# Half-size gather tables for the first pair, loads of x moved to GpSimd, and two extra matmuls before the first weight turn

## The chip, the cores and the metric

The kernel runs on one core of a Trainium2 chip. TensorE (PE) multiplies matrices, VectorE (DVE) and ScalarE (ACT) work on elements, GpSimd (POOL) issues the gathers, and SyncE (SP) and ACT issue plain transfers. The metric is device time in microseconds, lower is better: 733.51 us before the change (median of three runs, 733.4 to 733.7).

## The reference

Three layers of a compressed interaction network over B = 1024 rows, F = 39 fields, E = 64 embedding columns, H = 64 outputs a layer, all in float32:

```
def _cin_layer(Xk, X0, W, b):
    O = W.shape[0]
    Hk, Fdim = (Xk.shape[1], X0.shape[1])
    Wr = W.reshape(O, Hk, Fdim)
    return jnp.einsum('bhe,bfe,ohf->boe', Xk, X0, Wr) + b[None, :, None]
X0 = sparse_embedding
Xk = X0
outs = []
for W, b in ((W0, b0), (W1, b1), (W2, b2)):
    Xk = _cin_layer(Xk, X0, W, b)
    outs.append(Xk.sum(axis=-1))
cin_output = jnp.concatenate(outs, axis=-1)
return cin_output @ fc_w.T + fc_b
```

Only the sum over E of each layer and one dot product with fc_w leave the model, so the second and third layer can be folded into weights that act on products of two fields.

## The kernel before, in words

The 65,536 columns (b, e) are cut into 32 blocks of 2048. Every block needs products of pairs of fields. The products of a block fill six chunks of 128 rows (steps 0 to 5); what is left over, 32 rows of a half block, is done once for two blocks together, as step 6 of the even block (`join`). Two consecutive blocks are called a pair here; the first pair is blocks 0 and 1.

How a product is made: for each block GpSimd gathers five tiles of 128 rows of fields, `rt[n % 2][:, 0..4]`, out of a table in DRAM, by an indirect DMA with a column of row numbers from `lists` in SBUF (`gather_rows`, `roll`). VectorE multiplies two tiles (`product`, the pairs of tiles of steps 0 to 5 are (0,1), (0,2), (3,1), (3,2), (0,4), (3,4)), and TensorE multiplies the product by prepared weights and adds it up in PSUM (`multiply`: four matmuls of 512 columns a step). For step 6 the two tiles `ut` and `vt`, 128 rows of 1024 columns for a whole pair, are gathered by `roll_small`. At the end of a block ScalarE and VectorE combine its PSUM banks and add over E (`finish`).

The tables are `xd[0..2]` in DRAM, one for a pair: 40 rows for each of its blocks (39 fields and a row of ones), 2048 columns. `load(n)` fills the rows of block n from x, in runs of 64 elements. `fill_ones` writes the two rows of ones. `label` and `lists` say which field each gathered row holds.

The first block is treated apart. Its x arrives in two half tables `xh[0..1]` of 39 rows and 1024 columns by two transfers from ACT (`load_half`). GpSimd gathers tiles 0 to 3 of block 0 in halves out of them (eight half gathers); between the sixth and seventh it issues `load(1)` into `xd[0]`. SP copies the half tables into `xd[0]`, from where tile 4 of block 0 (`roll(0, (4,))`), then `ut`, `vt` (`roll_small(0)`) and the five whole tiles of block 1 (`roll(1)`) are gathered. Blocks 2 and 3 are loaded by SP in the main loop after step 0; from `n >= 2` on, SP loads block n + 4 when block n starts, and GpSimd loads blocks 4 and 5.

What sets the order: it is written out by hand, one instruction stream per engine, and an engine runs its stream in order. A gather that reads a table waits for the table's rows; a product waits for its tiles; a tile's next gather waits for the last product that reads it. The main loop runs VectorE four steps ahead of TensorE (`AHEAD = 4`), with four product buffers. `finish(0)` stands on VectorE's stream between the products of steps 3 and 4 of block 1. In the first block VectorE also builds the weights: `weight_rows(c)` (short additions, the rows of L526), and TensorE turns them (`weight_turn`), one chunk just ahead of its use. The turned weights come through ScalarE.

Before the main loop TensorE folds the weights: the matmuls of L406, L438, L418 and L487, with small matmuls of ones on a bank that nobody reads (`spin`) in between.

In `join` the rows of `p`, `ut` are four groups of 32 (t = 0 to 3). Group t holds block n + t // 2, half t % 2 of its columns. The row list for this comes from `seat` and `far`.

Of the kernel before, what the change touches and what calls it, by code (L numbers as in the profile page):

```python
# [66 lines left out]
NT = 5  # L67
# [8 lines left out]
MM = 512  # L76
SUB = 1024
# [5 lines left out]
BB = BLK // E  # L83
SB = SUB // E
NBLK = B // BB
NTAB = 3
# [61 lines left out]
def cin_kernel(ctx: ExitStack, tc: tile.TileContext, x, w0t, b0, w1, b1, w2, b2, fc_w, fc_b, out):  # L148
    nc = tc.nc
# [3 lines left out]
    const = ctx.enter_context(tc.tile_pool(name="const", bufs=1))  # L153
    dram = ctx.enter_context(tc.tile_pool(name="dram", bufs=1, space=DRAM))
# [3 lines left out]

    xv = x.rearrange("b f e -> f b e")
    xd = [dram.tile([2 * FT, BLK], F32, name=f"xd{k}") for k in range(NTAB)]  # L160
    xh = [dram.tile([F, SUB], F32, name=f"xh{k}") for k in range(2)]

    def bank(name):
        return psum.tile([128, MM], F32, name=name, tag="po")
# [1 line left out]
    def load(n, engine=nc.sync):  # L166
        first = n % 2 * FT
        engine.dma_start(  # L168
            xd[n // 2 % NTAB][first : first + F].rearrange("f (b e) -> f b e", e=E),
            xv[:, n * BB : (n + 1) * BB, :],  # L170
        )

    def gather_rows(dst, table, k):
        nc.gpsimd.indirect_dma_start(  # L174
            dst, None, table, bass.IndirectOffsetOnAxis(ap=lists[:, k : k + 1], axis=0)
        )

    def roll(n, tiles=range(NT)):
        for i in tiles:
            k = n % 2 * NT + i  # L180
            gather_rows(rt[n % 2][:, i], xd[n // 2 % NTAB][: FT if k < NT else 2 * FT], k)

    def roll_small(n):
        table = xd[n // 2 % NTAB].rearrange("f (t c) -> (f t) c", c=SUB)
        for k, dst in enumerate((ut, vt)):
            gather_rows(dst[n // 2 % 2], table, 2 * NT + k)

    wa = const.tile([128, NCHUNK, 3 * H], F32, name="wa")
    columns = const.tile([128, 3], F32, name="columns")
# [8 lines left out]
    wfin = const.tile([H + F, 1], F32, name="wfin")  # L198
    kfin = const.tile([NY * 32, 1], F32, name="kfin")

    lists = const.tile([128, 2 * NT + 2], I32, name="lists")
    rt = [const.tile([128, NT, BLK], F32, name=f"r{k}") for k in range(2)]
    ut = [const.tile([128, SUB], F32, name=f"u{k}") for k in range(2)]
    vt = [const.tile([128, SUB], F32, name=f"v{k}") for k in range(2)]
# [20 lines left out]
    with prep as prep:  # L225
# [24 lines left out]
        nc.sync.dma_start(fcrow, fc_w)  # L250
        def load_half(k):
            nc.scalar.dma_start(
                xh[k].rearrange("f (b e) -> b f e", e=E), x[k * SB : (k + 1) * SB]
            )

        nc.scalar.dma_start(w2s, w2.rearrange("o (s n) -> (o s) n", s=2))
# [20 lines left out]
        def spin(n=1, cols=MM // 2):  # L277
            for _ in range(n):
                nc.tensor.matmul(  # L279
                    idle[:, 0:cols],  # L280
                    nc.const_aps.tensor(1.0, (128, 128), F32),
                    nc.const_aps.tensor(1.0, (128, cols), F32),
                    start=True,
                    stop=True,
                )
# [1 line left out]
        spin()  # L287


        tmp = prep.tile([128, 16], F32, name="tmp")  # L290
# [77 lines left out]
        def fill_ones(k, engine, src):  # L368
            engine.dma_start(xd[k][F::FT].rearrange("r (p c) -> p r c", c=128), src)

        fill_ones(0, nc.gpsimd, ones)


        nc.vector.tensor_scalar(unit, apart, 0, None, ALU.is_equal)
        for h in (0, H):
# [4 lines left out]
        r, most, seat, far = (new() for _ in range(4))  # L380
# [6 lines left out]
        nc.vector.tensor_scalar(most, r, 23.0, 2.0, ALU.min, ALU.mult)  # L387

        halves = [slice(0, SUB), slice(SUB, BLK)]
        for k, cols in enumerate(halves):  # L390
            for i in range(4):
                gather_rows(rt[0][:, i, cols], xh[k], i)
                if k and i == 1:
                    load(1, nc.gpsimd)
        for k in (1, 0):
            nc.sync.dma_start(xd[0][0:F, halves[k]], xh[k])
        roll(0, (4,))

# [29 lines left out]
            )  # L428
        nc.vector.tensor_tensor(steps_at, steps_at, steps_by, ALU.mult)
        fused(seat, row, 96.0, seat, ALU.is_ge, ALU.add)  # L430
        step(row, 64.0, 2.0 * FT - 1.0, far)
        nc.vector.tensor_reduce(jumps, steps_at, AX.X, ALU.add)
        fused(most, r, 4.0, most, ALU.add, ALU.add)
        column = blocks.rearrange("h k (f j) -> h (k f) j", j=32)[:, :, 0]
# [26 lines left out]
        for k, n in enumerate((8, 5)):  # L461
            for t in range(2):
# [4 lines left out]
                        "h (a b s) -> h s a b", b=F, s=NW  # L467
                    ),
                )
        nc.vector.tensor_tensor(seat, seat, far, ALU.add)  # L470
        nc.vector.tensor_tensor(both_of[:, 0:1], most, jumps[:, 0:1], ALU.add)
        nc.vector.tensor_tensor(both_of[:, 1:2], both_of[:, 0:1], jumps[:, 1:2], ALU.add)
        nc.vector.tensor_scalar(lists[:, 2 * NT :], both_of, 2.0, seat, ALU.mult, ALU.add)
        roll_small(0)
        roll(1)
        for h in (0, H):
            nc.gpsimd.dma_start(b0s[h : h + H], b0.rearrange("(h o) -> h o", o=1))
        nc.gpsimd.dma_start(b1s, b1.rearrange("(h o) -> h o", o=1).to_broadcast([H, 2]))
# [1 line left out]
        nc.gpsimd.dma_start(  # L480
            fcb, fc_b.rearrange("(p o) -> p o", o=1).to_broadcast([NY * 32, 1])
        )
        fill_ones(2, nc.gpsimd, ones)
        w1v = w1s.rearrange("o (h f) -> o h f", f=F)
        groups = [(k, min(NA * k, F - NA)) for k in range(4)]
        for k, a in groups:
# [12 lines left out]
        for k, a in groups:  # L499
            new = NA * k - a  # L500
            rows = slice(NA * k, a + NA)
            copy = nc.scalar.copy if k < 3 else nc.vector.tensor_copy
            copy(bothv[H:128, rows, 0:32], flat[H:128, k, new:])
            if k > 1:
                first = slice(0, 3) if k == 2 else slice(k, k + 1)
                nc.scalar.copy(
                    bothv[H:128, NA * first.start : rows.stop, 32:FT].rearrange(
                        "h (k a) b -> h k a b", k=first.stop - first.start
                    ),
                    flat[0:H, first, new:, 0 : FT - 32],  # L510
                )
        first = [prods.tile([128, BLK], F32, name="p", tag="p") for _ in range(3)]


# [52 lines left out]
    def join(n, p):  # L567
        open_block(n + 1)

        def tiles(t, side):  # L570
            rows = slice(SQUARE * t, SQUARE * t + SQUARE)
            return rows, po[n + t // 2][2 * t % 4 + side]

        for side in range(2):
            for t in range(4):
                for half in range(2):
                    rows, dst = tiles(t, side)
                    at = (side + half) * H
                    nc.tensor.matmul(  # L579
                        dst[half * H : half * H + H],  # L580
                        wa[rows, NPAIR, at : at + H],
                        p[rows, bass.ts(side, MM)],
                        start=t >= 2,
                        stop=t < 2 and half == side,
                    )
        for t in range(4):
            for side in range(2):
                rows, dst = tiles(t, side)
                half = (1 - side) * H
                nc.tensor.matmul(  # L590
                    dst[half : half + H],
                    wa[rows, NPAIR + 1, H : 2 * H],
                    ut[n // 2 % 2][rows, bass.ts(side, MM)],
                    start=False,
                    stop=t < 2,
                )

    def fields(n):
# [61 lines left out]
    p = {}  # L660
# [26 lines left out]
        multiply(n, c, p[n, c], (1,))  # L687

    for at, (n, c) in enumerate(steps[:-TAIL]):
        if c == 0 and 2 <= n and n + 4 < NBLK:  # L690
            load(n + 4)
        quarters = range(BLK // MM)
        if at < 3:
            quarters = quarters[2:]
        if at < NPAIR and at > 1:
            multiply(n, c, p[n, c], quarters[:1])
            weight_turn(steps[at + 1][1])
            quarters = quarters[1:]
            if at == NPAIR - 1:
                multiply(n, c, p[n, c], quarters[:2])  # L700
                weight_turn(NPAIR + 1)
                quarters = quarters[2:]
        if c == NPAIR:
            join(n, p.pop((n, c)))
        else:
            multiply(n, c, p.pop((n, c)), quarters)
        if not at:
            fields(0)
            nc.scalar.copy(ones1, ones)
            fill_ones(1, nc.sync, ones1)  # L710
            for k in (2, 3):
                load(k)
        if at == NPAIR - 2:
            weight_rows(NPAIR + 1)
            for k in (NPAIR, NPAIR + 1):
                spread(k)
        if at - 1 in over:
            finish(over[at - 1])
            fields(over[at - 1] + 1)
        if at + AHEAD < len(steps):  # L720
            n, c = steps[at + AHEAD]
            if at + AHEAD <= NPAIR:
                weight_rows(c)
            p[n, c] = product(n, c)
            if c == NPAIR - 1 and n + 2 < NBLK:
                roll(n + 2)
                if n % 2 == 0:
                    roll_small(n + 2)
                if n < 2:
                    load(n + 4, nc.gpsimd)  # L730


# [73 lines left out]
```

## Time and profile before

| | before |
|---|---|
| median of the runs | 733.51 us (733.4 to 733.7) |
| the profiled execution | 733.14 us, of it 731.4 us span from first to last instruction |
| PE busy | 724.7 us, 99% of the span |
| DVE busy | 638.3 us, 87% |
| POOL busy (gathers and loads) | 397.6 us, 54% |
| ACT busy | 166.9 us, 23% |
| DMA moved | 197.24 MB, mean 270 GB/s |

The profile tells, for each engine, when it was busy and what ended its idle time. In the chain of waits one follows back from the last instruction what had to end before it; here it stays on TensorE from the first product matmul to the last. The first 45 us are therefore read by themselves: in the timelines of single engines, where each line is a start, a length, an engine, a source line, an operation and its tiles. For GpSimd the length of a gather is the time it takes to issue it, not the time until its data has landed.

### The profile page before, as it was taken

To read this page: it belongs to the slowest core of one execution; us is meant where nothing else is said; L and a number is where in the kernel's file an instruction comes from. 1 tells how busy PE (TensorE), PEld (TensorE's weight loads), DVE (VectorE), ACT (ScalarE), POOL (GpSimd) and SP (SyncE) were. 2 spreads that over 40 slices of the span, in tenths; PEclk is the share of its full clock that TensorE was granted. 3 is DMA by queue.
4 is the path that set the end of the run, shared out by engine and by line. 5 is a ranking of instruction groups with operands and counts; after the bars stand their busy time and mean duration, and the time that the engine had idled before them with its cause. 6 is when DMAs were issued, how large, how long until landed. Compare 5 with 4: busy or idle time off the path is not lost.

```text
span 731.4 us, 6351 instructions
## 1 busy us (share of the span) xinstructions
PE 724.7 (99%) x2375; PEld 316.1 (43%) x2375; DVE 638.3 (87%) x521; ACT 166.9 (23%) x240; POOL 397.6 (54%) x254
## 2 busy tenths in 40 slices
PE   8999999999999999999999999999999999999998
PEld 4444444444444444444444444444444444444443
DVE  6999798988889988889988889888898988889885
ACT  3332121222212222221222212222121221212222
POOL 6789886536555445754537555455654547545300
PEclk9999999999999999999999999999999999999999
DMA  8997899789575887757679675896767777565700
GB/s 268 376 337 280 315 342 356 290 307 338 232 273 231 281 336 286 270 225 285 269 288 330 223 289 219 304 348 236 268 256 274 301 287 266 224 252 236 288 0 0
DMA packets 65983, 197.24 MB, mean 270 GB/s; under 512 B 40110, under 2 KB 40179, under 8 KB 45984
## 3 DMA queue, kind: packets, MB, share of 16 engines
q0 software_dynamic: 28784, 185.56, 65.5%
q1 hardware_dynamic: 35468, 9.29, 5.5%
q10 hardware_dynamic: 1700, 1.99, 1.0%
q8 instruction: 18, 0.29, 0.1%
q14 instruction: 13, 0.11, 0.0%
HBM read 196.76 MB, written 10.60 MB: 284 GB/s over the span
## 4 chain that ended last, share of the span: by engine, by line
PE 99%; DVE 0%; DMA 0%; issue 0%; ACT 0%; DVEq 0%
PE po L559 91%; PE po L579 4%; PE po L590 2%; PE idle L279 0%; PE pv L406 0%; PE pt L487 0%; PE small L323 0%; PE pv L487 0%; PE pw L418 0%; DMA fcrow<-in_fc_w 0%; PE tr L543 0%; DVE g L609 0%; DVE pairs L526 0%; DVE sums L631 0%; ACT z L607 0%
## 5 line engine op out<-in xcount | busy, mean ns | idle before, releaser
L559 PE MATMUL po<-p,wa 128*128 128x512 f32 x1536 | 666.0, 594 | 0.0
L219 DVE TENSOR_TENSOR p<-r 128x2048 f32<-128x2048 f32 (+2 forms) x198 | 434.1, 2224 | 72.4 <-PE po L559 67.1
L559 PEld LDWEIGHTS po<-p,wa 128*128 128x128 f32 x1536 | 290.5, 190 | 371.7 <-issue 354.6
L174 POOL DMA_INDIRECT r<-xd,lists x156 | 302.3, 1938 | 267.1 <-issue 266.2
L607 ACT ACTIVATE z<-po,columns 64x512 f32<-64x512 f32 x128 | 87.3, 682 | 380.1 <-PE po L590 217.9
L609 DVE SCALAR_TENSOR_TENSOR g<-po,b0s,z 64x512 f32<-64x512 f32 x128 | 95.9, 749 | 9.3 <-ACT z L607 5.3
L602 ACT COPY g<-r 39x1024 f32<-39x1024 f32 x64 | 66.7, 1043 | 155.0 <-DVE sums L620 126.8
L620 DVE TENSOR_REDUCE sums<-g 103x16 f32<-103x1024 f32 x62 | 75.6, 1220 | 2.1
L174 POOL DMA_INDIRECT u<-xd,lists x16 | 38.9, 2432 | 7.5 <-issue 4.6
L174 POOL DMA_INDIRECT v<-xd,lists x16 | 38.5, 2403 | 4.9 <-issue 4.9
L579 PE MATMUL po<-p,wa 32*64 32x512 f32 x512 | 31.6, 600 | 0.0
L221 DVE TENSOR_TENSOR p<-u,v 128x1024 f32<-128x1024 f32 x16 | 19.5, 1218 | 0.0
L579 PEld LDWEIGHTS po<-p,wa 32*64 32x64 f32 x512 | 9.4, 131 | 20.2 <-issue 19.4
L590 PE MATMUL po<-u,wa 32*64 32x512 f32 x256 | 17.0, 587 | 0.0
L174 POOL DMA_INDIRECT r<-xh,lists x8 | 8.0, 996 | 4.8 <-DVE tmp L387 2.7
L590 PEld LDWEIGHTS po<-u,wa 32*64 32x64 f32 x256 | 5.7, 132 | 8.0 <-issue 8.0
L526 DVE TENSOR_TENSOR pairs<-both 128x2 f32<-128x2 f32 (+27 forms) x59 | 6.1, 171 | 0.2
L544 ACT COPY wa<-tr 128x128 f32<-128x128 f32 x8 | 2.1, 266 | 16.2 <-PE tr L543 16.2
L279 PE MATMUL idle<-const-float32-1.0 128*128 128x256 f32 (+1 forms) x8 | 4.0, 596 | 0.8 <-PEq L793 0.8
L543 PE MATMUL tr<-unit,pairs 128*128 128x128 f32 x8 | 2.4, 294 | 2.2 <-DVE pairs L526 2.2
L543 PEld LDWEIGHTS tr<-unit,pairs 128*128 128x128 f32 x8 | 1.2, 151 | 4.7 <-ACT pairs L524 2.7
L168 POOL DMA_DIRECT2D xd<-in_x x3 | 3.2, 1055 | 0.0
(97 smaller groups left out, 56.7 us busy)
## 6 DMA issues: line engine op xcount, KB each, us to landing
xd<-in_x SPq DMA_DIRECT2D x28, 312.0 KB
r<-xd,lists POOLq DMA_INDIRECT x156, 8.9
xd<-in_x POOLq DMA_DIRECT2D x3, 312.0 KB, 7.6
w2s<-in_w ACTq DMA_DIRECT2D x1, 624.0 KB
w1s<-in_w ACTq DMA_DIRECT2D x1, 624.0 KB
w0s<-in_w0t ACTq DMA_DIRECT2D x1, 380.2 KB
xh<-in_x ACTq DMA_DIRECT2D x2, 156.0 KB
xd<-xh SPq DMA_DIRECT2D x2, 156.0 KB
```

The costliest lines, as they stand in the source:

```text
L174: nc.gpsimd.indirect_dma_start(dst, None, table, bass.IndirectOffsetOnAxis(ap=lists[:, k : k + 1], axis=0))
L219: nc.vector.tensor_tensor(p[:, cols], r[:, i, cols], r[:, k, cols], ALU.mult)
L221: nc.vector.tensor_tensor(p[:, 0:SUB], ut[n // 2 % 2], vt[n // 2 % 2], ALU.mult)
L279: nc.tensor.matmul(idle[:, 0:cols], nc.const_aps.tensor(1.0, (128, 128), F32), nc.const_aps.tensor(1.0, (128, cols), F32), start=True, sto ...
L526: nc.vector.tensor_tensor(out, diagonal(a, b, sa, sb), diagonal(b, a, sb, sa), ALU.add)
L559: nc.tensor.matmul(po[n][m], wa[:, c, side : side + 2 * H], p[:, bass.ts(m, MM)], start=n % 2 == 0 and c == 0, stop=n % 2 == 1 and c == NP ...
L579: nc.tensor.matmul(dst[half * H : half * H + H], wa[rows, NPAIR, at : at + H], p[rows, bass.ts(side, MM)], start=t >= 2, stop=t < 2 and ha ...
L590: nc.tensor.matmul(dst[half : half + H], wa[rows, NPAIR + 1, H : 2 * H], ut[n // 2 % 2][rows, bass.ts(side, MM)], start=False, stop=t < 2,)
L602: nc.scalar.copy(gt[H : H + F], rt[n % 2][0:F, 0, bass.ts(m, SUB)])
L607: nc.scalar.activation(z[one], po[n][m][other], AF.Identity, bias=fc0s[other])
L609: return lambda: nc.vector.scalar_tensor_tensor(g[n][m // 2][0:H, at], po[n][m][one], b0s[one], z[one], ALU.add, ALU.mult)
L620: nc.vector.tensor_reduce(sums[:, b_at : b_at + SB], g[n][m // 2].rearrange("p (b e) -> p b e", e=E), AX.X, ALU.add,)
```

## The change

- The half tables `xh` now have 80 rows like `xd`, for both blocks of the first pair, and their own rows of ones. Block 1's two halves are loaded into them by two transfers from GpSimd after the eight half gathers. SP's two copies into `xd[0]` and `load(1)` are gone.
- Tile 4 of block 0 and all five tiles of block 1 are gathered in halves (`roll_half`). `ut` and `vt` of the first pair are gathered in two halves of 64 rows each.
- So that a half of `ut` lies in one half table, group t now holds block n + t % 2 and half t // 2, in every pair: the row lists and the bank and the start and stop flags in `join` follow.
- Blocks 2 and 3 are loaded by GpSimd, after block 1's gathers. Blocks 6 and 7 are loaded by GpSimd too, SP's loads begin with block 8. The ones of `xd[0]` are filled later, behind those of `xd[2]`.
- `spin(2, MM)`: two matmuls of 512 columns on the idle bank, between the matmuls of L487 and the first weight turn.

```
-    xh = [dram.tile([F, SUB], F32, name=f"xh{k}") for k in range(2)]
+    xh = [dram.tile([2 * FT, SUB], F32, name=f"xh{k}") for k in range(2)]
...
     def gather_rows(dst, table, k):
+        at = lists[0 : dst.shape[0], k : k + 1]
         nc.gpsimd.indirect_dma_start(
-            dst, None, table, bass.IndirectOffsetOnAxis(ap=lists[:, k : k + 1], axis=0)
-        )
+            dst, None, table, bass.IndirectOffsetOnAxis(ap=at, axis=0)
+        )
+
+    def roll_half(n, i, h):
+        k = n * NT + i
+        rows = F if n == 0 and i < NT - 1 else (n + 1) * FT
+        gather_rows(rt[n][:, i, bass.ts(h, SUB)], xh[h][0:rows], k)
...
     def roll_small(n):
-        table = xd[n // 2 % NTAB].rearrange("f (t c) -> (f t) c", c=SUB)
         for k, dst in enumerate((ut, vt)):
-            gather_rows(dst[n // 2 % 2], table, 2 * NT + k)
+            if n:
+                table = xd[n // 2 % NTAB].rearrange("f (t c) -> (f t) c", c=SUB)
+                gather_rows(dst[n // 2 % 2], table, 2 * NT + k)
+            else:
+                for h in range(2):
+                    gather_rows(dst[0][h * H : h * H + H], xh[h], 2 * NT + 2 + k)
...
-        fill_ones(0, nc.gpsimd, ones)
-
+        for k in range(2):
+            nc.gpsimd.dma_start(
+                xh[k][F::FT].rearrange("r (p c) -> p r c", c=128), ones[0:8]
+            )
...
         halves = [slice(0, SUB), slice(SUB, BLK)]
-        for k, cols in enumerate(halves):
-            for i in range(4):
-                gather_rows(rt[0][:, i, cols], xh[k], i)
-                if k and i == 1:
-                    load(1, nc.gpsimd)
-        for k in (1, 0):
-            nc.sync.dma_start(xd[0][0:F, halves[k]], xh[k])
-        roll(0, (4,))
+        for at in range(8):
+            roll_half(0, at % 4, at // 4)
+        for k in range(2):
+            nc.gpsimd.dma_start(
+                xh[k][FT : FT + F].rearrange("f (b e) -> f b e", e=E),
+                xv[:, BB + k * SB : BB + (k + 1) * SB, :],
+            )
+        for k in range(2):
+            roll_half(0, 4, k)
...
-        step(row, 64.0, 2.0 * FT - 1.0, far)
+        step(row, 64.0, 1.0 - 2.0 * FT, far)
...
-        nc.vector.tensor_tensor(seat, seat, far, ALU.add)
+        nc.vector.tensor_scalar(half_seat, seat, float(FT), None, ALU.mult)
+        fused(seat, seat, 2.0 * FT, far, ALU.mult, ALU.add)
...
-        nc.vector.tensor_scalar(lists[:, 2 * NT :], both_of, 2.0, seat, ALU.mult, ALU.add)
+        nc.vector.tensor_scalar(lists[:, 2 * NT + 2 :], both_of, half_seat, None, ALU.add)
+        nc.vector.tensor_scalar(
+            lists[:, 2 * NT : 2 * NT + 2], both_of, 2.0, seat, ALU.mult, ALU.add
+        )
         roll_small(0)
-        roll(1)
+        for i in range(NT):
+            for k in range(2):
+                roll_half(1, i, k)
+        for n in (2, 3):
+            load(n, nc.gpsimd)
...
-        fill_ones(2, nc.gpsimd, ones)
+        for k in (2, 0):
+            fill_ones(k, nc.gpsimd, ones)
...
+        spin(2, MM)
         first = [prods.tile([128, BLK], F32, name="p", tag="p") for _ in range(3)]
...
-            return rows, po[n + t // 2][2 * t % 4 + side]
+            return rows, po[n + t % 2][t // 2 * 2 + side]
...
-                        start=t >= 2,
-                        stop=t < 2 and half == side,
+                        start=t % 2 == 1,
+                        stop=t % 2 == 0 and half == side,
...
-                    stop=t < 2,
+                    stop=t % 2 == 0,
...
-        if c == 0 and 2 <= n and n + 4 < NBLK:
+        if c == 0 and 4 <= n and n + 4 < NBLK:
             load(n + 4)
...
             fill_ones(1, nc.sync, ones1)
-            for k in (2, 3):
-                load(k)
...
-                if n < 2:
+                if n < 4:
                     load(n + 4, nc.gpsimd)
```

More of the change, by code (lines that the diff above doesn't have):

```diff
@@ L199, in cin_kernel @@
     kfin = const.tile([NY * 32, 1], F32, name="kfin")
-    lists = const.tile([128, 2 * NT + 2], I32, name="lists")
+    lists = const.tile([128, 2 * NT + 4], I32, name="lists")
     rt = [const.tile([128, NT, BLK], F32, name=f"r{k}") for k in range(2)]
@@ L252, in load_half @@
             nc.scalar.dma_start(
-                xh[k].rearrange("f (b e) -> b f e", e=E), x[k * SB : (k + 1) * SB]
+                xh[k][0:F].rearrange("f (b e) -> b f e", e=E), x[k * SB : (k + 1) * SB]
             )
@@ L287, in cin_kernel @@
         spin()
-        tmp = prep.tile([128, 16], F32, name="tmp")
+        tmp = prep.tile([128, 18], F32, name="tmp")
         wide = prep.tile([128, 5, NT], F32, name="wide")
@@ L379, in cin_kernel @@
             )
-        r, most, seat, far = (new() for _ in range(4))
+        r, most, seat, far, half_seat = (new() for _ in range(5))
         both_of = prep.tile([128, 2], F32, name="both_of")
```

## The prediction

> **What bounds the kernel now.** The page gives PE 99% of the span, so I read the chain of waits first. Columns: start, length, what.
>
> ```profile
> 16.43 0.30 PE tr L543
> 16.73 0.61 PE idle L279 x2
> 17.34 1.82 PE po L559 x2
> 19.16 0.21 PE tr L543
> 19.38 2.23 PE po L559 x4
> 21.60 0.11 PE tr L543
> ...
> 43.06 41.40 PE po L559 x96
> ```
>
> From 17.34 us on the chain never leaves TensorE until the tail. The last line is steady state: 96 records are 12 steps, so a step takes 3.45 us and one record 0.431 us. The first six records took 1.82 + 2.23 = 4.05 us instead of 2.59: 1.46 us too long. The windows show why (PE busy, PEld, DVE, ACT, POOL, then PEclk, the granted clock):
>
> ```profile
> 15.00:16.00 1.00, 0.00 (x0) 0.00 (x0) 0.75 (x5) 0.53 (x3) 0.70 (x2) 1.00 0.76 287
> 16.00:17.00 1.00, 0.57 (x3) 0.36 (x3) 1.00 (x6) 0.23 (x2) 0.79 (x1) 0.93 1.07 377
> 19.00:20.00 1.00, 1.00 (x3) 0.51 (x2) 1.00 (x8) 0.38 (x2) 1.00 (x1) 0.50 1.07 365
> 20.00:21.00 1.00, 1.00 (x3) 0.51 (x2) 1.00 (x6) 0.00 (x0) 0.30 (x1) 0.86 0.99 360
> ```
>
> PE idles from 14.26 to 16.43 (2.18 us); at 16.86 (0.14 us of the second window at half) the clock halves, until 20.28.
>
> Then the engines that feed PE, in their timelines. VectorE (brackets: idle before):
>
> ```profile
> 26.78 2.35 DVE L219 TENSOR_TENSOR p<-r 128x1024 f32<-128x1024 f32 x2
> 29.77 2.28 DVE L219 TENSOR_TENSOR p<-r 128x2048 f32<-128x2048 f32 x1
> 32.88 2.28 DVE L219 TENSOR_TENSOR p<-r 128x2048 f32<-128x2048 f32 x1
> 37.22 2.29 DVE L219 TENSOR_TENSOR p<-r 128x2048 f32<-128x2048 f32 x1 [0.39 <-DMA r<-xd,lists]
> 42.42 4.50 DVE L219 TENSOR_TENSOR p<-r 128x2048 f32<-128x2048 f32 x2 [0.33 <-DMA r<-xd,lists]
> 52.35 11.09 DVE L219 TENSOR_TENSOR p<-r 128x2048 f32<-128x2048 f32 x5
> ```
>
> The line at 37.22 is step 0 of block 1, 42.42 its steps 2 and 3, 52.35 begins with step 4, behind finish(0). Each waits for a gathered tile. Step 4's product is ready at 52.35 + 2.28 = 54.6; PE wants it at 43.06 + 4 x 3.45 = 56.86. That slack, 2.2 us, is the smallest in block 1, and it is the number this change plays with. GpSimd:
>
> ```profile
> 24.47 0.95 POOL L174 DMA_INDIRECT v<-xd,lists  x1 [0.30 <-issue]
> 27.00 3.09 POOL L174 DMA_INDIRECT r<-xd,lists  x1 [0.30 <-issue]
> 30.39 2.61 POOL L174 DMA_INDIRECT r<-xd,lists  x1 [0.31 <-issue]
> 33.30 2.70 POOL L174 DMA_INDIRECT r<-xd,lists  x1 [0.30 <-issue]
> 36.30 1.34 POOL L174 DMA_INDIRECT r<-xd,lists  x1 [0.30 <-issue]
> 82.00 1.04 POOL L168 DMA_DIRECT2D xd<-in_x  x1
> ```
>
> A free gather takes 0.94 us plus 0.30 to the next, for 4 KB rows (u, v) as for 8 KB rows. The long ones end 0.8 to 0.95 us after the product that VectorE was running: 33.00 after 32.05, 36.00 after 35.16, 37.64 after 36.83. A plain load under a product (82.00) isn't stretched.
>
> [...] The shortest time to landing of a half gather here was 4.6 us, with other transfers beside it.
>
> **Part 1, the two dummies.** Four records of 0.431 us, 14.26 to 15.98, before the turn at 16.43, which waits for VectorE: they delay nothing at full clock, and the last L487 records are at full clock. The gap shrinks to 0.45 us and the clock should stay. PE then starts products about 0.2 us sooner and loses up to 1.46 us less. VectorE allows less: the third turn needs weight rows that end at 20.39, so it comes at 20.5 instead of 21.49 or so. Gain 1.0 us, if the later turns (rows done at 29.85) follow; that needs VectorE's 0.72 us wait at 22.66, for half 1 of tile 2, to go. It does: load(1) and SP's two copies (0.62 MB) no longer run ahead of that gather, and it is issued 1.1 us sooner. So PE would want step 0 of block 1 at 42.06 and step 4 at 55.86.
>
> **Part 2, the gathers of the first pair.** Before, from tile 4 of block 0 to tile 1 of block 1: 5 gathers, with a 2.9 us wait for block 1's load among them. Now 10, with half as many bytes each. Issue at 1.24 us: the eight halves end at 16.9, the two loads (at most 1.06 + 0.30 each) at 19.6, the first half of tile 4 at 20.9. From there VectorE, now without a wait, runs products 20.3 to 25.0 (four of 1.2), 26.0 to 28.4, 29.1 to 31.3, 32.2 to 34.4, 34.9 to 36.1 (step 6), with weight rows of 0.6 to 1.1 us between. A gather gets through at a product's end and takes 0.81 + 0.30, so the next falls into the next product: one gather a product. I let one through at every product's end: tile 4 21.5, u 22.7 and 23.8, v 25.0 and 27.2, tile 0 of block 1 28.4 and 31.3, tile 1 34.4 and 36.1, issued by 36.9. To landing I take 3.0 us from there[...]. So step 0 starts at 39.9 (39.3 to 40.5), against 37.22, and ends at 42.2. Tile 2 is issued meanwhile (37.2 to 39.4), tile 3's first half at 39.7, its second is held by step 0's product until 42.2, issued at 43.0, landed at 46.0 (44.8 to 47.2). Step 2 starts then, against 42.42, and step 4 is ready 12.2 us later, as before: 58.2. PE wants it at 55.86: a stall of 2.3 us, net 58.2 - 56.86 = +1.4 us (+0.2 to +2.5).
>
> Such a stall is as long as the gap that halved the clock before. I charge 1.5 us for that[...]. Sum: +2.9.
>
> **Part 3, the rest.** The copies and loads of SP that go were off the path; blocks 2 and 3, now loaded from 47 us or so (before 25.0), come in time unless block 2's gathers slip: step 0 of block 2 was made at 56.8 and wanted at 63.8, 7 us of cover; 0 to 2.4 us, I take 0. VectorE gets two short list instructions (0.15 us) near 9.9, ahead of an idle 1.55 us. The new order in join is the same 24 matmuls; block 0's last banks finish 0.2 us later, under VectorE's steps. ScalarE: nothing.
>
> The sum is against the profiled 733.14 us (span 731.4 and 1.7 around it), 0.4 below the median; the difference is put on the median: 733.51 + 2.9 = 736.4.
>
> **Rivals.**
> - *Hidden* (not slower). The gathers of 64 rows may need less than 0.81 us and pass in twos between products, and with the SP loads away from 25 us on tiles land sooner than I allow. If step 4 is ready by 55.86, only the gain stays: 733.51 - 1.0 = 732.5. It decides where tile 3's second half lands by 43.6. For it: the DMA engines no longer limit the stage. Against: the stretched gathers at 27.00 to 36.30. A small stall (up to 2.4 us, clock kept) also stays within 0.2%. [...]
> - *More gathers held*. Gathers often stay held across back-to-back products (27.00 spans two). Two more slots missed put tile 1 at about 43.6, PE stalls before step 0 as well, net about +5.5, with the clock 740 or so.
> - *The dummies harm*. If the clock is slow when they start they take 3.44 us, to 17.70, 1.3 us beyond the turn. Then +0.5 to +1.3 from them.
>
> **How the numbers follow.** This kernel can tell 0.2%, 1.47 us. Stall at step 4 as worked out: 0.48 (734 to 738, 0.06 of it inside 0.2%). Hidden or nearly: 0.33, of it 0.06 below 732.04. More gathers held: 0.16. Dummies harm without a stall: 0.03, same. Forecast 736.4; alone its range is 734 to 738. With the hidden case and the nearer half of the worst: 732.3 to 740.0. Faster 0.06, same 0.36, slower 0.58.
>
> **What would show it.** The first six product records at 2.6 us and a clock of 1.0 from 15 to 21 us show part 1. In GpSimd's timeline the gathers of block 1 should be 1.3 to 3 us long and tile 1's second half be issued near 36.9; step 0 of block 1 on VectorE near 39.9; in the chain a break of PE at step 4 near 56 us and a half-clock window behind it. I'm wrong if block 1's tiles land before 38 us, and the chain then stays on PE from 17 us on.

## The result, and the profile after

| | before | after |
|---|---|---|
| median of six runs each | 733.45 us (732.02 to 733.82) | 742.67 us (740.46 to 746.7) |
| the profiled execution | 733.14 us, span 731.4 us | 742.12 us, span 740.3 us |

The change makes the kernel slower: 1.0133 times the time, 95% interval 1.0105 to 1.0162. The forecast was 736.4 us with a range up to 740.0.

The chain of waits of the kernel after (start, length, what ended it or ran in it):

```profile
16.25 6.69 DMA r<-xh,lists
...
44.82 2.91 POOL r L175
...
52.51 1.98 DMA b0s<-in_b
54.50 2.97 issue
...
62.98 2.29 DVE p L229
65.32 27.73 PE po L582 x64
```

Before, the chain stayed on TensorE from 17.34 us on. Now it runs through GpSimd's gathers, a small load, `b0s`, and VectorE, and joins TensorE only at 65.32, which is step 4 of block 1. From there on TensorE waits no more. Step 4 began at 56.86 before, so 8.46 us of the 8.98 between the two profiled executions are lost in the first 65 us. TensorE's own timeline shows where they went:

```profile
15.34 1.13 PE L582 MATMUL po<-p,wa 128*128 128x512 f32 x2
...
16.66 1.96 PE L582 MATMUL po<-p,wa 128*128 128x512 f32 x4
...
40.35 1.06 PE L613 MATMUL po<-u,wa 32*64 32x512 f32 x16
46.98 17.05 PE L582 MATMUL po<-p,wa 128*128 128x512 f32 x32 [5.56 <-DVE p L229]
65.32 10.14 PE L582 MATMUL po<-p,wa 128*128 128x512 f32 x23 [1.29 <-DVE p L229]
```

The first six product records take about 3 us; the granted clock is 1.00 from 14 to 21 us. `join` of block 0 ends at 40.35 + 1.06 = 41.41, 1.64 us before its end in the kernel before (43.05). Then TensorE idles 5.56 us. Its 32 records up to step 4 take 17.05 us instead of 32 x 0.431 = 13.79, since the granted clock is 0.50 from 46.3 to 53.1 (0.66 in the window from 46 to 47 us, 0.50 in those up to 53, 0.93 from 53 to 54); that is 3.26. Then it waits 1.29 us for step 4. The sum, -1.64 + 5.56 + 3.26 + 1.29 = 8.47, is the whole loss.

VectorE's timeline tells what TensorE waited for:

```profile
35.01 1.23 DVE L231 TENSOR_TENSOR p<-u,v 128x1024 f32<-128x1024 f32 x1 [0.30 <-PE po L582]
44.63 2.29 DVE L229 TENSOR_TENSOR p<-r 128x2048 f32<-128x2048 f32 x1 [8.39 <-DMA r<-xh,lists]
...
50.00 4.49 DVE L229 TENSOR_TENSOR p<-r 128x2048 f32<-128x2048 f32 x2 [0.23 <-DMA r<-xh,lists]
57.46 1.53 DVE L632 SCALAR_TENSOR_TENSOR g<-po,b0s,z 64x512 f32<-64x512 f32 x2 [2.97 <-issue]
...
62.98 8.89 DVE L229 TENSOR_TENSOR p<-r 128x2048 f32<-128x2048 f32 x4
```

Step 0 of block 1 is made at 44.63 (37.22 before), steps 2 and 3 at 50.00 (42.42). Then VectorE stands still for 2.97 us ahead of finish(0), which reads `b0s`. The view calls this "issue", a wait without a releaser; but the two `b0s` loads were issued at 52.5 and 53.1 and landed 4.5 to 4.9 us later, between 57.0 and 58.0, and finish(0) begins at 57.46. Its other inputs, ScalarE's `z`, were done by 44.2. With these loads moved ahead finish(0) doesn't wait (`e7`, below, at 54.70), so I take it for a wait for `b0s`. And GpSimd's timeline tells why the tiles came late:

```profile
16.25 2.29 POOL L175 DMA_INDIRECT r<-xh,lists  x1 [0.30 <-issue]
...
20.56 2.07 POOL L175 DMA_INDIRECT r<-xh,lists  x1 [0.30 <-issue]
...
25.45 2.94 POOL L175 DMA_INDIRECT u<-xh,lists  x1 [0.31 <-issue]
...
29.90 1.94 POOL L175 DMA_INDIRECT v<-xh,lists  x1 [0.30 <-issue]
32.14 2.88 POOL L175 DMA_INDIRECT r<-xh,lists  x1 [0.30 <-issue]
35.32 1.74 POOL L175 DMA_INDIRECT r<-xh,lists  x1 [0.30 <-issue]
...
38.60 0.94 POOL L175 DMA_INDIRECT r<-xh,lists  x1 [0.30 <-issue]
...
52.51 1.23 POOL L498 DMA_DIRECT2D b0s<-in_b  x2
```

The line at 38.60 is the second half of tile 1. The gathers at 16.25, 20.56, 25.45, 29.90, 32.14 and 35.32 are stretched: each was issued under a product and ended 0.8 to 0.9 us after a product's end (35.02 after the product that ends at 34.17). One view shows what this does to the transfers, the windows from 22 to 38 us (last columns: granted clock, share of the DMA engines, GB/s), of the kernel before and then of the kernel after:

```profile
22.00:38.00 16.00, 16.00 (x42) 7.20 (x41) 14.84 (x44) 5.63 (x25) 12.95 (x8) 1.00 1.02 379
```

```profile
22.00:38.00 16.00, 15.93 (x40) 6.68 (x41) 13.32 (x42) 3.24 (x22) 13.56 (x9) 1.00 0.59 178
```

TensorE and GpSimd look alike in both. But the DMA engines, full before, are busy 59% of the time after and move 178 GB/s instead of 379: 2.8 MB in these 16 us instead of 6.1. Nine instructions of GpSimd fall into this stretch where eight did, and each of its gathers now brings half of what it did.

### The profile page after: what moved, and what is told of

It reads as the page before. It is cut to its first block, busy times and chain, and to the rows that moved or that the text cites. A ratio compares the mean times of both kernels' runs of the same rounds, so it can differ in the third digit from the quotient of the medians.

```text
span 740.3 us, 6371 instructions
## 1 busy us (share of the span) xinstructions
PE 727.6 (98%) x2379; PEld 315.1 (43%) x2379; DVE 639.0 (86%) x523; ACT 167.0 (23%) x240; POOL 408.7 (55%) x269
## 4 chain that ended last, share of the span: by engine, by line
PE 91%; POOL 4%; DVE 2%; issue 2%; DMA 1%; ACT 0%; DVEq 0%
PE po L582 85%; PE po L602 4%; POOL r L175 3%; PE po L613 2%; DMA r<-xh,lists 1%; POOL u L175 1%; DVE p L229 0%; DVE g L632 0%; POOL v L175 0%; DMA b0s<-in_b 0%; POOL xd L168 0%; PE small L333 0%; DVE sums L643 0%; DVE sums L654 0%; ACT z L630 0%
## 5 line engine op out<-in xcount | busy, mean ns | idle before, releaser
L175 POOL DMA_INDIRECT r<-xd,lists x150 | 294.6, 1964 | 263.3 <-issue 252.8
L175 POOL DMA_INDIRECT u<-xd,lists x15 | 34.7, 2313 | 4.6 <-issue 4.6
L175 POOL DMA_INDIRECT r<-xh,lists x20 | 28.0, 1402 | 7.8 <-issue 5.8
L175 POOL DMA_INDIRECT v<-xd,lists x15 | 28.8, 1920 | 4.6 <-issue 4.6
L602 PEld LDWEIGHTS po<-p,wa 32*64 32x64 f32 x512 | 9.4, 131 | 20.2 <-issue 20.2
L289 PE MATMUL idle<-const-float32-1.0 128*128 128x256 f32 (+2 forms) x12 | 5.7, 581 | 0.8 <-PEq L814 0.8
L168 POOL DMA_DIRECT2D xd<-in_x x6 | 6.3, 1061 | 0.0
L175 POOL DMA_INDIRECT u<-xh,lists x2 | 3.9, 1928 | 0.6 <-issue 0.3
L289 PEld LDWEIGHTS idle<-const-float32-1.0 128*128 128x128 f32 x12 | 2.6, 254 | 2.4 <-issue 2.2
```

Of the source, the lines that this page charges most:

```text
L168: engine.dma_start(xd[n // 2 % NTAB][first : first + F].rearrange("f (b e) -> f b e", e=E), xv[:, n * BB : (n + 1) * BB, :],)
L175: nc.gpsimd.indirect_dma_start(dst, None, table, bass.IndirectOffsetOnAxis(ap=at, axis=0))
L289: nc.tensor.matmul(idle[:, 0:cols], nc.const_aps.tensor(1.0, (128, 128), F32), nc.const_aps.tensor(1.0, (128, cols), F32), start=True, sto ...
L602: nc.tensor.matmul(dst[half * H : half * H + H], wa[rows, NPAIR, at : at + H], p[rows, bass.ts(side, MM)], start=t % 2 == 1, stop=t % 2 == ...
```

## The experiments

A ratio is to the kernel before, run beside it on the same chip, with its 95% interval. The profile shown of a run is one execution; the executions of one kernel here lie up to 6 us apart (the kernel before: 732.0 to 738.0 over 30 runs), so times and not single profiles decide. Even the start differs: among the profiles the first product record begins between 14.64 and 19.55 us, and the first four matmuls that fold w1, whose code is the same in both kernels, took 740 ns each in the kernel before and 452 in the kernel after (medians; without the dummies, in `e5`, 740 again), at a granted clock of 1.00 from 10 to 12 us in both kernels. Why is not shown. It is safer to count from the first product record: step 0 of block 1 comes 20.1 us after it in the kernel before and 29.3 us in the kernel after.

### The dummies and the new order in `join`

`e1_before_dummies`: the kernel before with the two dummies alone.

```
+        spin(2, MM)
         first = [prods.tile([128, BLK], F32, name="p", tag="p") for _ in range(3)]
```

> The kernel before with the two dummies of 512 columns alone. If the dummies do what the prediction's part 1 says, the clock stays full from 15 to 21 us and the time falls by 0.3 to 1.0 us (732.4 to 733.2)[...]. The rival (the dummies harm, because they overrun the turn) gives +0.5 to +1.3 us. In neither case do they explain +9 us.

Measured: 733.59 us, ratio 1.0000 (0.9986 to 1.0014). The profile, TensorE:

```profile
14.33 1.89 PE L279 MATMUL idle<-const-float32-1.0 128*128 128x512 f32 x4
...
17.34 1.12 PE L560 MATMUL po<-p,wa 128*128 128x512 f32 x2
...
43.40 14.00 PE L560 MATMUL po<-p,wa 128*128 128x512 f32 x32 [0.74 <-DVE p L219]
58.28 4.13 PE L560 MATMUL po<-p,wa 128*128 128x512 f32 x9 [0.88 <-DVE p L219]
```

The dummies (x4) fill the gap and the first six product records take about 3 us, as in the kernel after at its granted clock of 1.00. But this is the slowest of the 15 executions (738.92 us), and in it waits for VectorE follow, 0.74 us before step 0 of block 1 and 0.88 before its step 4: GpSimd's gather of `u` was held 4.34 us (21.81 to 26.15), where it took 0.94 before, and step 0 came at 41.05 instead of 37.22. How a usual execution loses the gain at the start, this profile can't show. No gain of 1.0 us is seen in the times; the interval leaves room for one of that size, no more.

`e5_after_no_dummies`: the kernel after without that `spin(2, MM)`.

> The changed kernel without the two dummies. Theory (step 4 of block 1 waits for VectorE, which does not depend on TensorE's clock before it): the same time as the changed kernel, 742.7 within 1.5, although TensorE runs at half clock earlier. Rival (the dummies take part in the loss): 735 or less.

Measured: 741.91 us, ratio 1.0118 (1.0077 to 1.0159). The clock is halved from 16.8 to 20.2 us in its profile, as before the change (mean granted clock of the profiled execution 0.993, in the kernel after 0.995), and the time is that of the kernel after within the intervals. The dummies are not what makes it slow, and no gain from them is seen.

`e4_before_join_order`: the kernel before with the new order of the row groups alone.

```
...
-            return rows, po[n + t // 2][2 * t % 4 + side]
+            return rows, po[n + t % 2][t // 2 * 2 + side]
...
-                        start=t >= 2,
-                        stop=t < 2 and half == side,
+                        start=t % 2 == 1,
+                        stop=t % 2 == 0 and half == side,
...
```

> The kernel before with the new order of the four row groups alone: row lists, banks, start and stop flags as in the changed kernel, in every pair. Theory: it costs nothing, 733.5 within 0.5. Rival (the order of the banks in the join delays each block's end): 0.2 us for each of 16 pairs, about +3 us.

Measured: 733.38 us, ratio 0.9993 (0.998 to 1.0006). It costs nothing that these times could show. What is left is the gathers and the loads.

### The number of gathers, and the products that hold them

`e3_before_five_more_gathers`: whole tables and whole tiles as before, and one more small gather (128 rows of 64 elements, from x) ahead of each tile of block 1.

```
...
-        roll(1)
+        for i in range(NT):
+            gather_rows(extra_rows[:, i], x.rearrange("b f e -> (b f) e"), NT + i)
+            roll(1, (i,))
```

> The kernel before with five more gathers of GpSimd, one ahead of each whole tile of block 1: 128 rows of 64 elements each into a tile that nobody reads (32 KB each, so hardly any data). Theory (the number of gathers counts, since VectorE's products hold most of them): tile 1 is issued two gathers later, some 3 to 6 us, and the time rises by 1 to 5 us (734.5 to 738.5). Rival (the half tables' data, 4 KB rows and their DMA, are slow, not the number of gathers): 733.5 within 0.4.

Measured: 738.94 us, ratio 1.0052 (1.0028 to 1.0075). Its GpSimd, then its VectorE:

```profile
29.54 2.62 POOL L174 DMA_INDIRECT extra_rows<-in_x,lists  x1 [0.30 <-issue]
32.47 2.68 POOL L174 DMA_INDIRECT r<-xd,lists  x1 [0.30 <-issue]
```

```profile
43.32 4.78 DVE L220 TENSOR_TENSOR p<-r 128x2048 f32<-128x2048 f32 x2 [7.33 <-DMA r<-xd,lists]
```

A gather of 32 KB is held under a product as long as a gather of 1 MB (2.62 us beside 2.68), and takes a place from it. Step 0 is made at 43.32, after 7.33 us of waiting for a tile. Not all of that is due to the extra gathers: in this execution, the slowest of seven, `u` was held 4.36 us ahead of them. The times decide: places alone, with hardly a byte more, cost about two fifths of what the change costs (0.52% of 1.33%, with an interval from 0.28 to 0.75%).

`e8_after_no_products`: the kernel after, but steps 3 to 5 of block 0 leave out the multiplication; ScalarE copies one of the two tiles in its place, so that VectorE runs no product from 25 to 34 us.

```
+            if n == 0 and c > 2:
+                nc.scalar.copy(p[:, cols], r[:, k, cols])
+            else:
+                nc.vector.tensor_tensor(p[:, cols], r[:, i, cols], r[:, k, cols], ALU.mult)
```

> The changed kernel, in which steps 3 to 5 of block 0 leave out the multiplication: ScalarE copies one of the two tiles instead, so that VectorE runs no product between 25 and 35 us (block 0's result is another). The number of gathers and their data stay. Theory (the products hold the gathers): the gathers of u, v and block 1 take 0.94 us each, tile 1 is issued by 33 to 35 us, step 0 of block 1 starts near 38 to 40 us, and 4 to 8 us go: 735 to 739. Rival (half tables, 4 KB rows, DMA): 742.7 within 1.

Measured: 738.93 us, ratio 1.0066 (1.0038 to 1.0094). GpSimd:

```profile
19.80 5.26 POOL L175 DMA_INDIRECT r<-xh,lists  x1 [0.30 <-issue]
25.37 0.92 POOL L175 DMA_INDIRECT u<-xh,lists  x1 [0.30 <-DVE pairs L552]
26.59 0.90 POOL L175 DMA_INDIRECT u<-xh,lists  x1 [0.30 <-issue]
...
33.95 0.94 POOL L175 DMA_INDIRECT r<-xh,lists  x1 [0.30 <-issue]
```

The gather at 19.80 falls under the products that are still there, and is held 5.26 us. From 25.37 on, with no product running until 34.51, every gather takes 0.89 to 0.95 us, and the second half of tile 1 is issued at 33.95 instead of 38.60. Step 0 of block 1 follows at 40.42 instead of 44.63. That is the direct proof that VectorE's products hold the gathers. It isn't the whole gain that it might be, since ScalarE's copies come late and TensorE then waits in block 0 (its `join` ends at 48.9).

`e6_after_whole_tiles`: the kernel after, with block 1's five tiles gathered whole out of a third table `xw`, which costs one more load; tile 4 of block 0, `ut` and `vt` stay in halves.

```
         for i in range(NT):
-            for k in range(2):
-                roll_half(1, i, k)
+            gather_rows(rt[1][:, i], xw, i)
```

> The changed kernel with block 1's five tiles gathered whole, five gathers instead of ten, out of a full-width table of block 1 that one more load of GpSimd fills (312 KB more to move, one more issue of 1.36 us). u, v and tile 4 stay in halves. Theory (number of gathers): step 0 of block 1 starts near 39 to 41 us instead of 44.6, the small loads are issued earlier too and finish(0) no longer waits for them, so 5 to 8 us go: 734.5 to 738. Rival (DMA traffic and latency): as slow as the changed kernel or slower, 742 to 744.

Measured: 741.38 us, ratio 1.009 (1.0065 to 1.0114): 1.3 us less than the kernel after by the medians, a third of the loss by the ratios, and less than I had expected. The two intervals overlap, so even this gain is not certain. GpSimd:

```profile
20.33 5.26 POOL L176 DMA_INDIRECT r<-xh,lists  x1 [0.30 <-issue]
25.89 2.87 POOL L176 DMA_INDIRECT u<-xh,lists  x1 [0.30 <-DVE pairs L553]
...
36.56 0.94 POOL L176 DMA_INDIRECT r<-xw,lists  x1 [0.30 <-issue]
37.81 0.95 POOL L176 DMA_INDIRECT r<-xw,lists  x1 [0.30 <-issue]
```

The loss is made before block 1 is reached. Four of the six half gathers of tile 4, `u` and `v` are held, 5.26, 2.87, 2.87 and 2.81 us, and block 1's first tile is issued at 36.56, when VectorE has no product left (25.73 before the change). Then whole tiles are too big: they are issued 1.25 us apart and land at the pace of the DMA engines, step 0 at 46.24.

`e11_before_three_in_halves`: the kernel before, with tile 4 of block 0, `ut` and `vt` in two gathers of 64 rows each.

```
...
-            gather_rows(dst[n // 2 % 2], table, 2 * NT + k)
+            (gather_rows if n else gather_halves)(dst[n // 2 % 2], table, 2 * NT + k)
...
-        roll(0, (4,))
+        gather_halves(rt[0][:, 4], xd[0][:FT], 4)
...
```

> The kernel before, with one part alone: tile 4 of block 0, u and v of the first pair are gathered in two halves of 64 rows each out of the whole table (6 gathers in place of 3, the same bytes; a second list for rows 64 to 127). Theory (a gather that falls under a product is held to its end, so what counts between 18 and 38 us is how many gathers there are and how many bytes each brings): three more places are needed ahead of block 1's tiles, most of them held 1.2 to 3 us; the DMA share between 22 and 38 us falls below 0.9 and step 0 of block 1 is made 3 to 6 us later than 37.2. TensorE stalls then 1 to 4 us: 735.5 to 739. Rival (the half tables, their loads by GpSimd and rows of 4 KB cost the time, not the count of gathers): none of that is here, so within 0.7 us of the kernel before.

Measured: 738.86 us, ratio 1.008 (1.0064 to 1.0096). The rival falls as the whole cause: block 1 has no half table here, tile 4 has its rows of 8 KB, none of the new loads is there, and yet over half of the loss is. Windows and GpSimd:

```profile
22.00:26.00 4.00, 4.00 (x11) 1.79 (x10) 2.00 (x2) 2.81 (x7) 3.39 (x3) 1.00 1.00 192
...
34.00:38.00 4.00, 4.00 (x11) 1.77 (x10) 4.00 (x14) 1.75 (x12) 3.39 (x3) 1.00 0.66 266
```

```profile
28.36 3.10 POOL L180 DMA_INDIRECT v<-xd,lists  x1 [0.31 <-issue]
...
34.71 2.69 POOL L174 DMA_INDIRECT r<-xd,lists  x1 [0.30 <-issue]
```

Tile 1 of block 1 (34.71) is issued 7.7 us later than before (27.00), and step 0 is made at 43.38. But the first of these windows shows a second thing: the DMA engines are full (share 1.00) at 192 GB/s, where the kernel before moved 408 GB/s in the same window at the same share. Gathers of 64 rows moved about half as much here, so the places are not the only cause.

`e12_before_block1_in_halves`: the same for block 1's five tiles alone.

```
...
-        roll(1)
+        for i in range(NT):
+            gather_halves(rt[1][:, i], xd[0][: 2 * FT], NT + i)
```

> The kernel before, with the other part alone: block 1's five tiles in two halves of 64 rows each out of the whole table (10 gathers in place of 5, the same bytes). Theory: tile 0 and tile 1 need four places under the products of block 0's steps 4 and 5 in place of two, and tiles 2 and 3 then come at half the bytes per place under block 1's own products; step 0 3 to 5 us later, 736 to 740, about what five more small gathers cost (738.9). Rival (VectorE is dry by 36 us, so the halves are then issued at 1.2 us each, 0.52 MB per 1.2 us, which is as fast as the DMA engines move them): at most 1.5 us slower, 733.5 to 735.5.

Measured: 742.86 us, ratio 1.0148 (1.0134 to 1.0163), beyond what either theory allowed. Windows, then VectorE:

```profile
38.00:42.00 4.00, 4.00 (x44) 1.54 (x49) 0.08 (x1) 0.38 (x2) 3.04 (x4) 1.00 1.00 221
42.00:46.00 4.00, 2.99 (x28) 1.09 (x12) 2.21 (x1) 0.82 (x2) 3.69 (x4) 1.00 1.03 229
46.00:50.00 4.00, 3.11 (x8) 1.24 (x7) 2.29 (x1) 1.91 (x3) 1.84 (x4) 1.00 1.03 227
```

```profile
41.92 2.29 DVE L227 TENSOR_TENSOR p<-r 128x2048 f32<-128x2048 f32 x1 [4.94 <-DMA r<-xd,lists]
46.51 2.29 DVE L227 TENSOR_TENSOR p<-r 128x2048 f32<-128x2048 f32 x1 [2.30 <-DMA r<-xd,lists]
51.14 4.49 DVE L227 TENSOR_TENSOR p<-r 128x2048 f32<-128x2048 f32 x2 [2.34 <-DMA r<-xd,lists]
```

From 38 us all gathers but one are issued freely (0.9 us each), the DMA engines are full (share 1.00 to 1.03), and yet only 221 to 229 GB/s are moved, not the rival's 0.52 MB in 1.2 us, 433 GB/s, which whole tiles did reach in `e3` (433 from 42 to 46 us, at a share of 1.03): one tile in 4.6 us, and VectorE waits 2.3 us for each. This run measures the rate of gathers of 64 rows, not the holding, and says nothing of the number of places. In the changed kernel only `ut` and `vt` of the first pair are gathered in 64 rows.

### The small loads

`e2_after_small_loads_early`: the kernel after, with `b0s`, `b1s`, `b2s` and `fcb` loaded by SP at the start instead of by GpSimd behind the loads of blocks 2 and 3.

```
         nc.sync.dma_start(fcrow, fc_w)
+        for h in (0, H):
+            nc.sync.dma_start(b0s[h : h + H], b0.rearrange("(h o) -> h o", o=1))
...
-        for h in (0, H):
-            nc.gpsimd.dma_start(b0s[h : h + H], b0.rearrange("(h o) -> h o", o=1))
...
```

> The changed kernel with the five small loads (b0, b1, b2, fc_b) issued by SP at the start instead of by GpSimd behind block 1's gathers and the loads of blocks 2 and 3. Theory: VectorE's idle 2.97 us before finish(0) is a wait for b0s, and it stands on the path to step 4 of block 1, so 2.5 to 3.0 us go: 739.7 to 740.2. Rival (TensorE's two half-speed windows cost the time, and the wait for b0s only fills it): no more than 0.5 us goes.

Measured: 742.98 us, ratio 1.0122 (1.0088 to 1.0157): no gain. VectorE of its profiled execution:

```profile
40.58 1.22 DVE L231 TENSOR_TENSOR p<-u,v 128x1024 f32<-128x1024 f32 x1 [3.35 <-DMA v<-xh,lists]
48.09 2.29 DVE L229 TENSOR_TENSOR p<-r 128x2048 f32<-128x2048 f32 x1 [6.29 <-DMA r<-xh,lists]
...
57.62 1.52 DVE L632 SCALAR_TENSOR_TENSOR g<-po,b0s,z 64x512 f32<-64x512 f32 x2
```

There is no wait ahead of finish(0) any more. But the edit did more than it was meant to, as ACT's issues of `w0s` show, in the kernel after and then here:

```profile
1.85 0.83 ACTq L268 DMA_DIRECT2D w0s<-in_w0t  x1
```

```profile
4.90 0.58 ACTq L275 DMA_DIRECT2D w0s<-in_w0t  x1
```

With the small loads on SP, ACT's loads of `w0s`, w1 and the second half of x went out 2.8 us later or more (`e7` shows it too, no other run does; why is not shown). TensorE waited 1.30 us for w1, the first product record began at 19.55 instead of 15.34, the gathers of `u` and `v` were held behind that, and step 0 came at 48.09. So this run does not price the wait for `b0s`. TensorE's sum above does, for that one execution, and with step 0 at its old place little was to be had: TensorE itself reached step 4 only 1.29 us before VectorE had it, being idle and then at half clock until 53.1. The wait for `b0s` lies beside those, and its removal alone could have brought 1.29 us there at most. A gain of that size would not show in these intervals.

`e7_after_whole_tiles_small_early`: the edits of the whole tiles and of the early small loads together.

> The run before with the five small loads by SP at the start as well. Theory: what is left of the wait for b0s goes, 0 to 1 us less than the run with whole tiles alone, 734 to 737.5. If finish(0) still waited there, up to 3 us less.

Measured: 741.66 us, ratio 1.0111 (1.0077 to 1.0145), which is that of `e6` and of the kernel after within the intervals. Its profiled execution was its fastest (739.19): two halves of tile 4 held 4.93 and 2.93 us, step 0 at 45.30, finish(0) without a wait. With both later terms removed, the held half gathers ahead of block 1 remain. That they alone are enough isn't shown, since `w0s` is issued late here as well (4.62).

### A kernel that does better than both?

If GpSimd's places are scarce, one should be taken from it. `e9_before_load1_by_act`: the kernel before, with block 1's load on ScalarE's queue behind the half loads; `e10_before_load1_by_act_dummies`: the same with the dummies.

```
         load_half(1)
+        load(1, nc.scalar)
...
-                if k and i == 1:
-                    load(1, nc.gpsimd)
```

> The kernel before, with one edit: block 1's load goes out on ScalarE's queue behind the two half loads, instead of on GpSimd's between the sixth and seventh half gather. The whole tables and the count of gathers stay. My theory (GpSimd's place between VectorE's products is the scarce thing in the first 45 us): GpSimd is one load issue (1.06 us) shorter and need not wait for that load at 20.3 to 23.2, so tile 4, u and v are issued 1 to 3 us sooner and step 0 of block 1 is made at 35 to 37 us instead of 37.2 to 39; step 4 has more slack. Time 731.5 to 733.5, at most 2 us gained, since TensorE still starts its products at 17.1 and loses a half clock at 17 to 20 us. Rival (bytes on the DMA engines are what limits the head): the load, moved ahead, collides with the half loads and the eight half gathers; first product 0.5 to 2 us later, 734 to 736.

> As the run beside it, with the two dummies of 512 columns as well. Theory: the dummies bring the 1.0 us that my prediction gave them only if VectorE and the tiles can follow; with block 1's tiles earlier the waits of 0.74 and 0.88 us that took the gain back go, so this is 0.5 to 1.2 us faster than the same kernel without the dummies: 730.5 to 732.5. Rival: the later waits are VectorE's own weight rows and products, not tiles; then the dummies again change nothing (within 0.4 us of the kernel beside it).

Measured: 734.06 us, ratio 0.9994 (0.9975 to 1.0012), and 735.94 us, ratio 1.002 (1.0006 to 1.0033). The first kernel's executions fall between 731.41 and 736.63. In its profiled one (731.69) tile 1 is issued at 24.82 and step 0 made at 35.41, 1.8 us earlier than before the change, and TensorE then never waits until 99.27. That looks like what was foretold, but the whole start of this execution is early:

```profile
14.64 2.01 PE L558 MATMUL po<-p,wa 128*128 128x512 f32 x2
```

The first product record began at 17.14 in the kernel before. Counted from it, tile 1 is issued after 10.2 us (9.9 before) and step 0 made after 20.8 (20.1 before): no gain in the profile either. With the dummies it isn't faster but if anything slower: in the profiled execution no tile is waited for in block 1, and TensorE waits 2.27 us before the third weight turn (23.06), which the profile puts down to VectorE's product. Why that turn came so late, 2.2 us after its weight rows were done at 20.81, isn't settled. Neither beats the kernel before.

## Why the prediction was wrong

The sign and the place were right: gathers of the first pair are held by products, block 1's tiles come late, and VectorE's step 4 sets the loss. The size was wrong by the terms of part 2 and by a wait, for `b0s`, that part 3 had left out.

- *Part 1, the dummies.* The granted clock stayed at 1.00 from 14 to 21 us and the gap before the turn shrank to 0.58 us, as foretold. The gain of 1.0 us was not seen where the dummies stand alone (ratio 1.0000); where a usual execution loses it is open. In the kernel after the first product record begins 1.8 us earlier than before, but that is the early start of this execution and not the dummies, which stand behind the matmuls that ran faster (with the dummies alone, in `e1`, it began at 17.34). All of it is lost again in the idle 5.56 us.
- *A plain load under a product.* The load at 82.00 that I gave for this ran ahead of a product, which began at 82.80. The statement holds all the same: in the kernel after two loads that begin at 50.57 lie under products (50.00 to 54.49) and took 2.08 us together.
- *"I let one through at every product's end".* This is the step that failed first. The eighth half gather of block 0, which I had ended at 16.9, was held under a product until 18.5. Among the three products from 20.51 to 24.18 gathers did get through, but under the two from 25.14 to 27.49, which follow each other at once, the gather stayed held to the end of the second (25.45 for 2.94 us, released 0.9 us after 27.49). The first half of tile 0 was issued by 35.0 where the list of places gave 29.2. Then VectorE ran dry, gathers were free, and the second half of tile 1 was issued by 39.5 instead of 36.9: +2.6 us.
- *"To landing I take 3.0 us".* This was my estimate, and no trace showed it. It took 5.1 (39.54 to 44.63): once VectorE is dry, half a tile is issued each 1.24 us, 0.42 MB a microsecond, and the DMA engines, starved until 38 us, moved 0.28 (38 to 42 us) to 0.35 (42 to 46 us, at a share of 1.02). I read this as transfers queueing behind each other. +2.1, so step 0 came at 44.63 instead of 39.9. Part of it is made good by then: step 2 began at 50.00 instead of 46.0, +4.0.
- *What was missed.* The move of loads in part 3 was priced for blocks 2 and 3 only. The small loads stand behind them in GpSimd's order: `b0s` was issued 14.9 us later than before (52.5 against 37.64), and finish(0), which was to follow step 3 at once, waited 2.97 us: the 3.0 us that the sum lacked. I had not walked down the queue that the loads were put on.
- *The clock.* I charged 1.5 us. The granted clock was 0.50 for 6.8 us from 46.3 on, but VectorE had step 4 only at 65.3, so that on this path the halved clock cost nothing. With it left out, 1.4 + 4.0 + 3.0 = 8.4 is VectorE's account of the 8.46 us.
- *The rivals.* "More gathers held" was the one that came: I gave it 0.16 and priced it at 740, without `b0s`. "Hidden" and "the dummies harm" are refuted by the traces and by `e1` and `e5`. For the first I had said that the DMA engines no longer limit the stage; the profile has them at 0.59, and that was not a relief but the mark of the trouble.

Shown are: that products hold the gathers (`e8`: 0.89 to 0.95 us each with none running, 5.26 us under them), that further gathers cost time even when they carry hardly anything (`e3`: 0.52%), that the dummies and the order in `join` cost nothing that could be seen. The share of `b0s` is read from one profile and no run prices it. Nor does a run separate the number of gathers from the rate of gathers of 64 rows (192 GB/s in `e11`) in `ut` and `vt`, since `e11` holds both. For the kernel after its profile speaks for the number:

```profile
34.00:35.00 1.00, 1.00 (x4) 0.52 (x3) 0.71 (x8) 0.22 (x2) 1.00 (x1) 1.00 0.00 0
```

In this microsecond the DMA engines moved nothing (last two columns): tile 4, `u` and `v` had landed while the first half of tile 0 was still held, to 35.02. So in this execution the rate of `u` and `v` did not delay block 1's tiles.

## What to carry to other kernels

Where GpSimd issues gathers beside an engine that holds them, count the gathers as places between the products and ask how many bytes a place brings: halving the transfers halved what the whole stage moved here (379 to 178 GB/s), and a DMA share that falls while the issuing engine stays as busy is the sign (1.02 to 0.59). When a transfer is moved to another queue, go down that queue to its end and find who waits for the smallest thing on it. And where two waits lie side by side, as `b0s` beside an idle and half-clocked TensorE, price each by what is late next, not by its length. Before two profiles are compared, look whether they start alike, and whether an edit that moves a load has moved others with it, as in `e2`.

## What was not expected of the hardware

- Gathers of 64 rows kept the DMA engines as full as gathers of 128 and moved about half: 221 to 229 GB/s at a share of 1.00 to 1.03 in `e12` (38 to 50 us), where whole tiles move 405 at 1.02 in the kernel before (38 to 42 us). Why is not shown.
- The price of an idle TensorE does not follow the length of the gap alone. After 2.18 us of idle the granted clock was 0.50 for 3.4 us in the kernel before (16.86 to 20.28), after 2.49 us (at 45.7 us in `e3`) it stayed at 1.00 (42 to 54 us), and with 5.56 us in the kernel after it was 0.50 for 6.8 us, from 46.3 on, before the gap had ended at 46.98. What else it follows is not shown.
- A held gather can outlast several products that follow each other at once, and does not always. Where VectorE ran the four products near 20 us without a pause, the gather issued among them was held to the end of the fourth in seven profiles (from 3.62 us in `e2` to 5.26 in `e5`, `e6` and `e8`), while in `e10` gathers got through in between. In the profiles in which VectorE paused among the four for a tile (0.72 us in the kernel before, 0.75 after), none was held over 2.9 us there. A wait of VectorE that looks like a loss may thus be the gap that lets a gather out; no run tests this by itself.
